# A fused LayerNorm, graph and GRU layer on one core: a planner's clock that follows tiles and loads, and a seven-product scheme in 30 batches instead of 24

## The chip, the cores and the metric

The kernel runs on 1 core of a Trainium2 chip, in one launch. The metric is device time in microseconds (us) of that core, lower is better. TensorE (PE) is the matrix engine, VectorE (DVE) and ScalarE (ACT) the elementwise engines, GpSimd (POOL) and SyncE (SP) mostly issue transfers here. "PEld" in the profile is the load of PE's stationary operand.

## What is computed

The reference, cut to what matters (32 batches of 512 rows with 256 channels, all fp32):

```python
h = maximum(layernorm(x), 0)
# inside the layer, with x standing for h:
c = relu(bn1(conv1d(xc, conv1_w)));  c = bn2(conv1d(c, conv2_w, taps=17, pad=8))
x_conv = relu(c + xc)                          # xc is x, transposed
s = x @ w_se.T + b_se                          # 3 columns
A = exp(-|s_n - s_m|^2) * adj
x_nmp = A @ relu(x @ w_msg.T + b_msg)
x_in = concat(x_conv, x_nmp)
r = sigmoid(x_in @ Wi_r + x @ Wh_r);  z = sigmoid(x_in @ Wi_z + x @ Wh_z)
n = tanh(x_in @ Wi_n + r * (x @ Wh_n))
out = x_before + (1 - z) * n + z * x
```

## The kernel before

The program is written out by Python at build time. Five generators ("streams") each yield pieces of work: `rows` (the 1x1 convolution), `begins` (LayerNorm and transposition), `graphs` (adjacency part), `conv` (the 17-tap convolution, as a fast-convolution scheme of 25 products in each of 7 groups of columns) and `gates` (the GRU). A loop at the end of the kernel function (from L1672) plays planner: it keeps a clock `now`, which is the modelled time of PE's front, and for each of ACT and DVE an `Engine` object with a modelled `free` time. A stream yields the time from which its next piece may be issued; the loop issues the piece of the stream that is furthest behind among those that are ready, adds its matmuls' modelled time to `now`, and goes on. If no stream is ready, `now` is advanced by 0.25 us, and in the early part (before the first gate batch is loaded) every fourth such empty step issues a transposition that only keeps PE busy (`keep_warm`, L147). Elementwise work with no deadline (`background`, `fill`) is issued whenever DVE's modelled backlog is under 1.5 us. All engines then run this written order[...]. The planner's times decide only the order; a wrong time shows as an engine that waits.

The clock of the version before is coarse. `Engine.issue` (L126) adds a fixed cost and a cost per element, from `max(self.free, now)`; it doesn't ask whether the inputs are there. `LAG`, 0.6 us, is added to an engine's free time wherever PE depends on it. Transfers have fixed times: a load of weights is taken to land at `now + 7.0`, of a batch's transposed rows (`load_row`) at `now + 8.0`, of a mask at no time at all.

PE's matmuls are all recorded at L137 (`matmul`), the transpositions at L142 (`turn`), the small matmuls of the adjacency kernel at L983 (`kernel_exp`), elementwise work at L128 (the `Engine` wrapper). An fp32 matmul stands as two records in the profile.

The gates of one batch are two units (`unit(o)`, o = 0, 1: halves of the output channels). A plain unit issues 18 matmuls of 512 columns: 6 each for the r, z and n gates. A "fast" unit computes the r and z products of the hidden and the convolution inputs with a seven-product scheme on halves (`term`: 7 terms of 2 matmuls of 256 columns), in place of 8 matmuls of 512, and keeps the other 10 matmuls of 512. The scheme needs sums of its data (`data_sums`, six DVE operations a batch) and of its weights (`weight_sums`, once). Within a fast unit:

- three terms fill `ps_r`'s two halves and `ps_z`'s first half; ACT copies `ps_r`'s second half to `fifth` (128x256)
- `spread(ps_r, 0)` brings `ps_z`'s first half plus `fifth` into `ps_r`'s second half
- one more term goes onto `ps_z`'s first half, and `spread(ps_z, 1)` brings that half plus `fifth` into `ps_z`'s second half
- the remaining terms and the matmuls on the graph input follow, then ACT takes tanh of `ps_r` and `ps_z`.

`spread` in the version before looks at DVE's modelled time. With `SOON = -1` it issues the sum on DVE only if DVE has been free for over 1 us. Otherwise ACT copies `ps_z`'s half, and the `fifth` is "owed": `settle_owed` adds it on DVE just before the tanh, with the tanh issued 0.2 us after that. Between the pieces stand matmuls of the unit before (`some_new`: the n gate's last four, `NEW`) and of this one (`hidden`).

Fast batches are `FIRST_FAST <= b < B - PLAIN`: with `PLAIN = 7` batches 1 to 24, so 24 of 32.

Of the kernel before, what the change touches and what calls it, by code (L numbers as in the profile page):

```python
# [13 lines left out]
P = 128  # L14
# [36 lines left out]
def kernel(  # L51
# [43 lines left out]
    const = ctx.enter_context(tc.tile_pool(name="const", bufs=1))  # L95
    front = ctx.enter_context(tc.tile_pool(name="front", bufs=2))
    cv = ctx.enter_context(tc.tile_pool(name="cv", bufs=1))
    dram = ctx.enter_context(tc.tile_pool(name="dram", bufs=1, space=bass.MemoryType.DRAM))
    acc = ctx.enter_context(tc.tile_pool(name="acc", bufs=3, space=PSUM))
    gps = ctx.enter_context(tc.tile_pool(name="gps", bufs=3, space=PSUM))  # L100
    first_ctx = ExitStack()
    cps = first_ctx.enter_context(tc.tile_pool(name="cps", bufs=2, space=PSUM))
    ctx.enter_context(tc.manual_schedule())
    late = None

    now = 5.0
    LAG = 0.6
# [6 lines left out]

    class Engine:
        def __init__(self, engine, fixed, each):
            self.engine, self.fixed, self.each, self.free = engine, fixed, each, 0.0

        def behind(self, other):
            self.free = max(self.free, other.free + 0.1)

        def __getattr__(self, name):
            def issue(*tiles, **more):
                size = max(elements(t) for t in tiles if hasattr(t, "shape"))  # L126
                self.free = max(self.free, now) + self.fixed + self.each * size
                getattr(self.engine, name)(*tiles, **more)  # L128

            return issue  # L130

    dve, act = Engine(nc.vector, 0.12, 0.00108), Engine(nc.scalar, 0.16, 0.0009)

    def matmul(ps, lhsT, rhs, **more):
        nonlocal now
        now += max(0.223, 0.005 + elements(ps) / 600.0)
        nc.tensor.matmul(ps, lhsT, rhs, **more)  # L137

    def turn(ps, a):
        nonlocal now  # L140
        now += 0.11
        nc.tensor.transpose(ps, a, ident)  # L142

    def keep_warm(n):

        for _ in range(n):
            nc.tensor.transpose(unused[:, :P], ident, ident)  # L147
# [22 lines left out]
    def store_at(t, dst, src):  # L170
        todo = [lambda: nc.gpsimd.dma_start(dst, src)]

        def run():
            if todo:
                todo.pop()()

        STORES.append(run)
        later(t, run)
# [8 lines left out]
    ARRIVES = (0.0, 7.0, 11.0, 13.0)  # L187
# [6 lines left out]
    def fetch(b, xs=None):  # L194
        XS[b] = front.tile([P, NT, D], F32, name="x_sb", bufs=2) if xs is None else xs
        step = NT // 2 if b == 0 else NT
        for c in range(0, NT, step):
            nc.sync.dma_start(
                XS[b][:, c : c + step], x[b].rearrange("(c p) d -> p c d", p=P)[:, c : c + step]
            )  # L200

    def load(b, xs=None):
# [3 lines left out]
        NORM_AT[b] = max(now + 7.0, 50.0) if b >= G else ARRIVES[b]  # L206

    def load_row(b):
        if b not in HR:
            settle_stores()  # L210
            HR[b] = front.tile([P, ND, N], F32, name="hT", bufs=2)
            nc.sync.dma_start(HR[b], HD[b])
            HR_AT[b] = now + 8.0

    def load_graph(b):
        if b < B and b not in HG and begun > b:
            settle_stores()
            HG[b] = front.tile([P, ND, N], F32, name="hTg", bufs=1)
            nc.sync.dma_start(HG[b], HD[b])

    def load_gates(b):
# [4 lines left out]
        nc.sync.dma_start(HB[b], HD[b])  # L226
        HB_AT[b] = now + 8.0

    def load_conv(b):

        if b < B and b not in XC and evacuated.get(b, 1e9) <= now:
            XC[b] = late.tile([P, ND, N], F32, name="xconv", bufs=2)
            nc.sync.dma_start(XC[b], CD[b])
            XC_AT[b] = now + 7.0
# [14 lines left out]
    def load_sums(b, d):  # L249
        if b < B and (b, d) not in XN:  # L250
            settle_stores()
            XN[b, d] = late.tile([P, N], F32, name="xnb", bufs=2)
            nc.sync.dma_start(XN[b, d], ND_[b, d])
            XN_AT[b] = now + 6.0
# [3 lines left out]
    vec = const.tile([P, _NCOL], F32)  # L258
    nc.sync.dma_start(vec, vecs)
    w1 = const.tile([P, ND, D], F32)  # L260
    nc.sync.dma_start(w1, conv1_w)

    prep_ctx = ExitStack()
    prep = prep_ctx.enter_context(tc.tile_pool(name="prep", bufs=1))
    wraw = prep.tile([P, ND, 2, 3, 3, D], F32)
    nc.gpsimd.memset(wraw[:, :, 0, 0, 0, :], 0.0)
# [3 lines left out]
    wmsg = const.tile([P, ND, D + 3], F32)  # L270
    bmsg = const.tile([P, D + 3], F32)
    ident = const.tile([P, P], F32)
    make_identity(nc, ident)
    mhalf = const.tile([P, 4], F32)
    nc.gpsimd.memset(mhalf, -0.5)

    def rsqrt(dst, var):
# [4 lines left out]
        nc.gpsimd.tensor_tensor(dst, t[:, :n], mhalf[:, :n], op=ALU.pow)  # L282
# [15 lines left out]
    h1 = const.tile([P, Q * RV], F32)  # L298
# [4 lines left out]
    def zeros(g):  # L303
        at = input_of(g)
        for b in range(B + 1):
            v = U * b - STARTS[g]
            if 0 <= v <= sizes(g)[0]:
                nc.gpsimd.memset(at[:, : Q if v == sizes(g)[0] else LEAD, :, v : v + 1], 0.0)
                if v > 0:
                    nc.gpsimd.memset(at[:, Q - 1 : Q, :, v - 1 : v], 0.0)  # L310
# [3 lines left out]
    class Graphs:  # L314


        def __init__(self):
# [6 lines left out]
            nc.gpsimd.memset(self.aug, 1.0)  # L324
            nc.gpsimd.memset(self.augr, 0.0)
            nc.gpsimd.memset(self.augl, -1.0)
# [3 lines left out]
        def ask(self, more):  # L330
# [3 lines left out]
            for k in range(self.asked, min(self.asked + more, NT * B)):  # L334
# [3 lines left out]
                if b < TURNED:  # L338
                    nc.sync.dma_start(m, adj[b, c * P : (c + 1) * P, :])
                for g in range(P // 32 if b >= TURNED else 0):  # L340
                    at = c * P + 32 * g
                    nc.sync.dma_start(
# [37 lines left out]
    def norm_some(b):  # L380

        if now < NORM_AT[b]:
# [144 lines left out]
    PLAIN = 7  # L527
# [8 lines left out]
    def weights_first():  # L536
# [10 lines left out]
        for j1 in ORDER:  # L547
# [12 lines left out]
            for j2 in ORDER:  # L560
# [7 lines left out]
                for k in range(2):  # L568
# [4 lines left out]
                    nc.scalar.dma_start(WD[len(WS)][:, k], w[k])  # L573
# [4 lines left out]
    def weights_again():  # L578


        for m in range(25, 25 * NG):
            W_BASE.append(taken)
            w = {}
            for k in (1,) if m % 25 == LONE else (2, 0, 1):
                yield
                w[k] = new_w()
                if k < 2 or m >= 50:
                    nc.sync.dma_start(w[k], WD[m % 25][:, k])
            WS.append(w)
            W_AT.append(now + 7.0)  # L590
# [10 lines left out]
    def third_weight(m):  # L601
# [5 lines left out]
        later(dve.free + 0.4, lambda: nc.gpsimd.dma_start(WD[m % 25][:, 2], w[2]))  # L607
# [103 lines left out]
    def evacuate():  # L711
# [10 lines left out]
        if g == 0 and b < 2:  # L722
# [10 lines left out]
            if o == ND - 1:  # L733
                evacuated[b] = XC_AT[b] = act.free + 0.7 + LAG
# [7 lines left out]
        act.free += 0.7  # L742
        PARTS.append(act.free + 5.0)
        n0, n1 = Q * first, min(Q * last, N)
        later(act.free + 0.4, lambda: nc.gpsimd.dma_start(CD[b][:, o, n0:n1], part[:, : n1 - n0]))
        if o == ND - 1 and last == U:
            evacuated[b] = PARTS[-1]
        return True

    AHEAD, SOON = 3, -1  # L750
# [31 lines left out]
    def prepare_some():  # L782
        nonlocal prepare_at
        if len(WS) >= 25 or len(WS) >= at_product + 3 or now < prepare_at:
# [4 lines left out]
    def convolution():  # L789
# [28 lines left out]
        for g in range(NG):  # L818
# [3 lines left out]
            if g == 1:  # L822
                first_ctx.close()
                cps = ctx.enter_context(tc.tile_pool(name="cps2", bufs=1, space=PSUM))
# [3 lines left out]
            for n in range(25):  # L828
# [6 lines left out]
                if late is None and len(WS) >= 25:  # L835
# [48 lines left out]
    def late_pools():  # L884
        nonlocal late, wih, whh, wsum, tsum
        prep_ctx.close()
        late = ctx.enter_context(tc.tile_pool(name="late", bufs=1))
        whh = late.tile([P, ND, 3 * D], F32, name="whh")
        wih = late.tile([P, 2 * ND, 3 * D], F32, name="wih")
        nc.sync.dma_start(whh, w_hh)  # L890
        nc.sync.dma_start(wih, w_ih)
# [80 lines left out]
    def kernel_exp(at):  # L972

        nonlocal now, bank_at, exp_waits
# [6 lines left out]
        for c in range(NT):  # L981
            k = slice(32 * c, 32 * c + 5)
            nc.tensor.matmul(  # L983
# [3 lines left out]
        now += 1.15  # L987
# [33 lines left out]
    def blocks(t, rows, o):  # L1021
        for g in range(P // 32):
            at = o * P + 32 * g
            nc.sync.dma_start(
# [11 lines left out]
    def begin(b):  # L1036
# [4 lines left out]
        if b >= TURNED:  # L1041
# [3 lines left out]
            nc.gpsimd.dma_start(XD_[b].rearrange("(c p) d -> p c d", p=P), xs)  # L1045
            yield now + 7.0
# [3 lines left out]
            yield now + 8.0  # L1050
# [8 lines left out]
            nc.gpsimd.dma_start(HD[b], HT[b])  # L1059
# [9 lines left out]
        for d in range(ND):  # L1069
            norm_t(b, d)  # L1070
# [6 lines left out]
    def rows(g, b):  # L1077
        nonlocal made, made_at
        for o in range(ND):
            conv1(g, b, o)  # L1080
# [5 lines left out]
    def graph(b):  # L1086
# [3 lines left out]
        if b == 0:  # L1090
            HG[0] = HT[0]
            yield act.free + LAG
        elif b not in HG:
            load_graph(b)
            yield now + 9.0
        msg = front.tile([P, NT, D], F32, name="msg", bufs=1)
        for c in range(NT):
            messages(b, msg, c)
            yield now
        told = b + 1  # L1100
        factors()
        yield dve.free + LAG
# [11 lines left out]
        for n in range(NT):  # L1114
            masked(b, at, n)
# [4 lines left out]
        for d in range(ND):  # L1120
            gather(b, msg, at, d)
# [4 lines left out]
    def gates(b):  # L1126
# [4 lines left out]
        if b < B - 1:  # L1131
            nc.sync.dma_start(out[b], x[b])
        else:
            nc.sync.dma_start(out[b][:, :P], x[b][:, :P])
# [3 lines left out]
        if b == 0:  # L1138
            yield now + 8.0
# [70 lines left out]
        def store(y, o, s):  # L1210
            for g in range(P // 32):
# [3 lines left out]
                if is_last(o):  # L1215
                    (nc.scalar if g % 2 else nc.sync).dma_start(dst, src)
                else:
                    nc.gpsimd.dma_start(dst, src, accum_op=ALU.add)  # L1218

        fast = FIRST_FAST <= b < B - PLAIN  # L1220
        if b == B - PLAIN:
            for w, at in ((whh, w_hh), (wih, w_ih)):
                nc.sync.dma_start(w[:, 0, D : 2 * D], at[:, 0, D : 2 * D])
# [484 lines left out]
```

## Time and profile before

| | |
|---|---|
| median of 3 runs (lowest to highest) | 2067.28 us (2066.85 to 2071.51) |
| profiled execution's own time, its span | 2067.35 us, 2065.6 us |
| PE, DVE, ACT, POOL busy | 2012.4, 1416.3, 888.4, 451.1 us |
| mean granted TensorE clock | 0.989 |
| DVE `ps_acc<-ps_acc,fifth`, 128x256, x96 | 41.1 us, 428 ns each |
| ACT `ps_acc<-ps_acc`, 128x256, x122 | 45.9 us, 376 ns each |
| ACT `fifth<-ps_acc`, 128x256, x48 | 18.4 us, 384 ns each |
| start of the last convolution product, of the last adjacency product (`ps_g<-at,msg`) | 1844.2, 1852.5 us of the span |

"Span" runs from the first to the last instruction on the core. A group of the page has its line, engine, operation, the tile written and those read, the shape and the count, then busy time and mean duration. The list of PE's waits names what PE waited for: the time in total, how often, and the longest single one.

### The profile page before, as it was taken

Reading aid. Unit: us, or ns where it says so; the run is one execution under the profiler, and the core shown is the slowest. Engines: PE = TensorE matmul, PEld = TensorE weight load, DVE = VectorE, ACT = ScalarE, POOL = GpSimd, SP = SyncE. Lnnn points to the kernel's source line nnn. Section 1 sums busy time; section 2 is a strip of 40 time slices with the busy share of each in tenths; the row PEclk is TensorE's granted clock in tenths of the full one; section 3 lists DMA queues with packets and bytes.
Section 4 is the critical chain, followed back from the end, with each engine's and each line's share of the span. In section 5 each row is a group of like instructions: output and inputs, shape, how many; then the busy total and the mean of one; then the engine's idle time right before and its main releaser. Section 6 shows DMA issues by size and latency. Waiting matters only on the chain. (4 is left out here: it accounts for less than half of the span.)

```text
span 2065.6 us, 27386 instructions
## 1 busy us (share of the span) xinstructions
PE 2012.4 (97%) x9199; PEld 1360.9 (66%) x9199; DVE 1416.3 (69%) x2626; ACT 888.4 (43%) x1805; POOL 451.1 (22%) x578
## 2 busy tenths in 40 slices
PE   8999889999999999999999999999999999999998
PEld 4878556676676766677577676667775677664444
DVE  6789378885878848687587775677875777752223
ACT  6554454335543445433454334554334633334221
POOL 2101022321212213122141221231221311114222
PEclk9999999999999999999999999999999999999999
DMA  7455668898979869778789788797886776756554
GB/s 286 150 174 184 225 209 196 192 226 226 223 197 203 190 192 205 201 182 212 183 193 223 172 204 206 164 197 204 207 204 175 189 158 159 173 118 143 63 92 36
DMA packets 581227, 378.70 MB, mean 183 GB/s; under 512 B 457648, under 2 KB 475344, under 8 KB 579952
## 3 DMA queue, kind: packets, MB, share of 16 engines
q1 hardware_dynamic: 419616, 279.02, 49.1%
q0 software_dynamic: 153184, 84.70, 23.9%
q10 hardware_dynamic: 8288, 13.24, 1.7%
q8 instruction: 73, 1.20, 0.2%
q14 instruction: 66, 0.54, 0.1%
HBM read 278.81 MB, written 114.56 MB: 190 GB/s over the span
## 5 line engine op out<-in xcount | busy, mean ns | idle before, releaser
L1218 POOL DMA_DIRECT2D out_dram<-o_sb x252 | 275.9, 1718 | 659.1 <-DVE o_sb L128 628.9
L137 PE MATMUL ps_acc<-xnb,wih 128*128 128x512 f32 (+1 forms) x772 | 364.4, 593 | 0.7 <-DVE ps_acc L128 0.7
L137 PEld LDWEIGHTS ps_c<-xd,w 128*128 128x128 f32 x2304 | 288.6, 191 | 55.0 <-issue 38.9
L137 PEld LDWEIGHTS ps_c<-x,w 128*128 128x128 f32 x2032 | 258.4, 193 | 72.3 <-issue 49.2
L137 PE MATMUL ps_c<-xd,w 128*128 128x135 f32 (+1 forms) x2304 | 291.8, 280 | 7.0 <-ACT ps_c L128 7.0
L137 PE MATMUL ps_c<-x,w 128*128 128x135 f32 (+2 forms) x2032 | 267.4, 281 | 11.4 <-ACT n L128 5.0
L137 PE MATMUL ps_acc<-hTb,whh 128*128 128x512 f32 (+2 forms) x580 | 239.5, 523 | 0.4 <-ACT r L128 0.4
L137 PE MATMUL ps_acc<-xconv,wih 128*128 128x512 f32 (+1 forms) x580 | 238.9, 519 | 0.3 <-DVE ps_acc L128 0.3
L137 PE MATMUL ps_g<-at,msg 128*128 128x512 f32 x512 | 227.1, 593 | 0.8 <-DVE at L128 0.8
L137 PEld LDWEIGHTS ps_acc<-xnb,wih 128*128 128x128 f32 x772 | 142.6, 191 | 115.6 <-issue 108.7
L137 PEld LDWEIGHTS ps_g<-at,msg 128*128 128x128 f32 x512 | 95.4, 190 | 106.4 <-issue 101.1
L137 PEld LDWEIGHTS ps_acc<-xconv,wih 128*128 128x128 f32 x580 | 107.6, 190 | 74.9 <-issue 67.5
L137 PEld LDWEIGHTS ps_acc<-hTb,whh 128*128 128x128 f32 x580 | 104.8, 191 | 78.6 <-issue 71.2
L128 DVE TENSOR_TENSOR msg<-ps_g,bmsg 128x256 f32<-128x256 f32 x128 | 53.7, 420 | 143.5 <-PE ps_g L137 143.1
L128 DVE SCALAR_TENSOR_TENSOR x<-x,x 128x544 f32<-128x544 f32 (+5 forms) x161 | 137.5, 854 | 2.9
L128 DVE TENSOR_TENSOR o_sb<-hTb,r 128x512 f32<-128x512 f32 x63 | 43.3, 687 | 124.1 <-ACT r L128 123.5
L128 ACT ACTIVATE ps_c<-ps_c 128x270 f32<-128x270 f32 (+1 forms) x144 | 56.1, 389 | 167.8 <-PE ps_c L137 167.8
L128 DVE TENSOR_TENSOR x<-x 128x272 f32<-128x272 f32 (+5 forms) x280 | 127.4, 497 | 0.2
L137 PE MATMUL ps_g<-hT,w 128*128 128x512 f32 (+8 forms) x296 | 122.1, 560 | 3.7 <-DMA hT<-hd 2.5
L137 PE MATMUL ps_g<-wmsg,hTg 128*128 128x259 f32 x496 | 123.5, 382 | 0.7 <-DVE aug L128 0.7
L128 ACT ACTIVATE h<-ps_g,bn_shift,bn_scale 128x252 f32<-128x252 f32 (+8 forms) x212 | 86.5, 485 | 73.2 <-PE ps_g L137 73.2
L128 DVE TENSOR_TENSOR xd<-x 128x544 f32<-128x544 f32 (+1 forms) x144 | 102.5, 716 | 14.0 <-PE ps_c L137 13.7
(149 smaller groups left out, 2927.5 us busy)
## 6 DMA issues: line engine op xcount, KB each, us to landing
w<-wd SPq DMA_DIRECT2D x414, 256.0 KB, 3.4
m_sb<-in_adj_dram SPq DMA_DIRECT2D x384, 64.0 KB, 3.8
hT<-hd SPq DMA_DIRECT2D x33, 512.0 KB, 4.4
hd<-hT POOLq DMA_DIRECT2D x32, 512.0 KB, 5.5
hTb<-hd SPq DMA_DIRECT2D x32, 512.0 KB, 4.6
xnb<-nd SPq DMA_DIRECT2D x64, 256.0 KB, 3.0
out_dram<-o_sb POOLq DMA_DIRECT2D x252, 64.0 KB, 4.9
hTg<-hd SPq DMA_DIRECT2D x31, 512.0 KB, 4.3
```

The source lines that it names most:

```text
L128: getattr(self.engine, name)(*tiles, **more)
L137: nc.tensor.matmul(ps, lhsT, rhs, **more)
L1218: nc.gpsimd.dma_start(dst, src, accum_op=ALU.add)
```

## The change

It does four things.

1. The clock. Every tile pool is wrapped in a `Pool`, every engine, POOL and SP included, in an `Engine`; each instruction and transfer records which part of which tile it wrote or read, and when that ends in the model (`note`). An instruction's modelled start is then the latest of its engine's free time and its tiles' times (`after`), PE's included (`on_pe`: `now` moves forward to the time at which operands are there). Durations have new constants. A transfer's modelled landing comes from an issue time, a latency and a shared rate (`Engine.dma_start`), and the loads' fixed 6, 7 and 8 us give way to `done(tile)`. `LAG` goes from 0.6 to 0.17.
2. The streams wait for more: for a free PSUM bank of the ring (`gps.free("ps_g")`) ahead of each use of one, for masks to have landed, for a free `hT` buffer ahead of a row load; LayerNorm pieces and weight preparation are held back while ACT's modelled backlog is over 0.5 us (`BUSY`); the late pools open when the preparation's tiles are modelled to be done within 1 us.
3. `spread` always issues the sum on DVE, at once behind the term in the program; the copy on ACT and `settle_owed` are gone.
4. `PLAIN` goes from 7 to 1: batches 1 to 30 are fast.

The diff, cut to its core:

```diff
-    now = 5.0
-    LAG = 0.6
+    now = 0.0
+    LAG = 0.17
+    BUSY = 0.5
+    HAND = 0.04
+    def after(who, outs, ins):
+        at = 0.0
+        for a in ins:
+            for k, end in met(a.tensor.name, region(a)):
+                if k[4]:
+                    at = max(at, end if k[5] == who else end + HAND)
+        for a in outs:
+            at = max(at, BORN.get(a.tensor.name, 0.0))
+            for k, end in met(a.tensor.name, region(a)):
+                if k[5] != who:
+                    at = max(at, end + HAND)
+        return at
...
     class Engine:
-        def __init__(self, engine, fixed, each):
-            self.engine, self.fixed, self.each, self.free = engine, fixed, each, 0.0
...
+        def dma_start(self, dst, src, **more):
...
+            at = max(self.free, after("DMA", [dst], [src]), lanes[0])
+            if name == "P":
+                issue = 1.1 if run < 512 else 0.78 if run == 1024 else 0.55
+            else:
+                issue = 0.53 if run < 512 else 0.43 if run == 1024 else 0.37
+            self.free = at + issue
+            rate = 150e3 if run < 512 else 330e3
+            flow = (self.free + 1.85, 4 * elements(dst) * dst.shape[0] / rate)
...
             def issue(*tiles, **more):
-                size = max(elements(t) for t in tiles if hasattr(t, "shape"))
-                self.free = max(self.free, now) + self.fixed + self.each * size
-                getattr(self.engine, name)(*tiles, **more)
+                some = [t for t in tiles if hasattr(t, "ap")]
+                given = [v for k, v in more.items() if k in ("bias", "scale") and hasattr(v, "ap")]
+                at = max(self.free, after(self.name, some[:1], some[1:] + given))
+                wide = some[0].ap[-1][0] > 8 and self.name == "ACT"
+                each = self.each * (2.2 if wide else 1.0)
+                fixed = 0.13 if op == "memset" else self.fixed
+                self.free = at + fixed + each * max(elements(t) for t in some) + 0.1 * len(given)
+                note(self.name, some[:1], some[1:] + given, self.free + self.tail)
+                getattr(self.engine, op)(*tiles, **more)
...
-    dve, act = Engine(nc.vector, 0.12, 0.00108), Engine(nc.scalar, 0.16, 0.0009)
+    dve, act = Engine("DVE", nc.vector, 0.066, 0.00106, 0.085), Engine("ACT", nc.scalar, 0.05, 0.00087, 0.12)
+    pool, sp = Engine("POOL", nc.gpsimd, 1.1, 0.0003, 0.0), Engine("SP", nc.sync, 0.0, 0.0, 0.0)
+    def on_pe(out, ins, took):
+        nonlocal now
+        now = max(now, after("PE", [out], ins)) + took
+        note("PE", [out], ins, now + 0.163)
...
-            HR_AT[b] = now + 8.0
+            HR_AT[b] = done(HR[b])
...
-        if now < NORM_AT[b]:
+        if now < NORM_AT[b] or act.free > now + BUSY:
             return False
...
-    PLAIN = 7
+    PLAIN = 1
...
-            W_AT.append(now + 7.0)
+            W_AT.append(done(*(w.values() if isinstance(w, dict) else [w])))
...
-                if late is None and len(WS) >= 25:
+                if late is None and len(WS) >= 25 and prep.over() <= now + 1.0:
                     late_pools()
...
         for c in range(NT):
+            yield gps.free("ps_g")
             messages(b, msg, c)
-            yield now
...
-                def spread(ps, k):
-                    if dve.free < now + SOON:
-                        yield max(now, fifth_at)
-                        dve.tensor_tensor(ps[:, hi], ps_z[:, lo], fifth, op=ALU.add)
-                        return dve.free + 0.3
-                    yield now
-                    act.activation(ps[:, hi], ps_z[:, lo], AF.Copy)
-                    owed.add(k)
-                    return act.free + LAG
-
-                def settle_owed(ps, k, then):
-                    if k not in owed:
-                        then()
-                        return
-                    dve.tensor_tensor(ps[:, hi], ps[:, hi], fifth, op=ALU.add)
-                    later(dve.free + 0.2, then)
+                def spread(ps):
+                    dve.tensor_tensor(ps[:, hi], ps_z[:, lo], fifth, op=ALU.add)
+                    return dve.free + LAG
...
-                r_at = yield from spread(ps_r, 0)
+                r_at = spread(ps_r)
+                yield now
...
-                z_at = yield from spread(ps_z, 1)
+                z_at = spread(ps_z)
+                yield now
...
-                yield from products(ps_z, o, 1, (2,), lambda: settle_owed(ps_z, 1, update), clear=False)
+                yield from products(ps_z, o, 1, (2,), update, clear=False)
```

## The prediction

> **What bounds the kernel now.** I read the page's busy times first, then the same busy times by stretch, PE's waits, and last the timeline at the places that they point to.
>
> ```profile
> span 2065.6 us, 27386 instructions
> ...
> PE 2012.4 (97%) x9199; PEld 1360.9 (66%) x9199; DVE 1416.3 (69%) x2626; ACT 888.4 (43%) x1805; POOL 451.1 (22%) x578
> ```
>
> PE is busy for 97% of the span: 53.2 us are idle, and no other engine comes near. So the time is PE's work, plus the idle time, plus what PE does at a reduced clock. By stretch (length, then busy time of PE, PEld, DVE, ACT, POOL, then granted clock, DMA share and GB/s):
>
> ```profile
> 0.00:52.00 52.00, 45.00 (x156) 25.84 (x157) 32.07 (x92) 32.39 (x71) 11.55 (x33) 0.93 0.77 286
> 52.00:310.00 258.00, 237.31 (x1419) 181.73 (x1419) 188.49 (x393) 132.06 (x283) 30.40 (x50) 0.96 0.56 188
> 310.00:1033.00 723.00, 707.53 (x3338) 494.10 (x3337) 546.11 (x990) 316.13 (x660) 161.06 (x210) 0.99 0.84 202
> 1033.00:1860.00 827.00, 823.45 (x3815) 569.89 (x3814) 594.07 (x1072) 354.57 (x721) 185.75 (x223) 1.00 0.79 184
> 1860.00:2014.00 154.00, 154.00 (x360) 68.27 (x359) 39.60 (x55) 43.67 (x55) 49.30 (x50) 1.00 0.59 100
> 2014.00:2066.00 52.00, 45.11 (x117) 21.10 (x116) 15.92 (x27) 9.55 (x15) 13.02 (x12) 0.98 0.41 35
> ```
>
> Idle PE, length less busy: 7.0, 20.7, 15.5, 3.6, 0 and 6.9 us. The first and last rows are loading at the start and the last unit's elementwise work; I leave both alone. What a better order can win lies between 52 and 1860 us: 39.8 us. The waits of PE from 310 to 1033 us (total, times, longest) name the releasers:
>
> ```profile
> PE ps_c L983 <- ACT z L128: 6.7, 3, 4.0
> PE ps_c L137 <- ACT ps_c L128: 3.6, 3, 3.1
> PE ps_c L137 <- ACT z L128: 1.7, 1, 1.7
> PE ps_g L137 <- DMA hT<-hd: 1.2, 1, 1.2
> ```
>
> It is ACT's evacuations, held up in ACT's own list. Two rows of ACT's waits over the whole run, and the worst place, on ACT and PE:
>
> ```profile
> ACT z L128 <- DVE ps_acc L128: 38.4, 21, 3.8
> ...
> ACT r L128 <- DVE ps_acc L128: 26.9, 13, 4.9
> ```
>
> ```profile
> 837.17 4.43 ACT L128 ACTIVATE y<-z 128x1620 f32<-128x1620 f32 x3
> ...
> 841.63 0.68 ACT L128 ACTIVATE z<-ps_c 128x270 f32<-128x270 f32 x2
> ...
> 842.37 1.22 PE L983 MATMUL ps_c<-right,left 5*128 5x512 f32 x1 [4.01 <-ACT z L128]
> ```
>
> The two rows of waits are the owed sums: ACT stands before a tanh until DVE has added `fifth`, 65.3 us in 34 cases, and everything behind it on ACT stands too. The timeline shows three copies of 1.5 us ahead of the evacuation that frees PE's bank: PE waited 4.0 us there.
>
> [...] one late sum holds ACT for up to 4.9 us. [...] behind the 4.0 us wait, at 842 us, the two pairs of small matmul rows start 1.01 us apart, against 0.53 us at 785 us, and the clock column is under 1.00 in just the stretches with waits. [...] The trace has 428 for the sum from PSUM, and I use that.
>
> **The change, part by part**
>
> *Six more fast batches.* In the timeline, two 512-column matmuls (four records) start 1.72 us before what follows, so 0.86 us each; one of 256 columns (two records) 0.43 us:
>
> ```profile
> 1103.10 0.59 PE L137 MATMUL ps_acc<-hTb,whh 128*128 128x256 f32 x2
> 1103.53 0.59 PE L137 MATMUL ps_acc<-xconv,wih 128*128 128x256 f32 x2
> ```
>
> ```profile
> 2033.13 1.88 PE L137 MATMUL ps_acc<-xnb,wih 128*128 128x512 f32 x4
> 2034.85 1.88 PE L137 MATMUL ps_acc<-hTb,whh 128*128 128x512 f32 x4
> ```
>
> A plain unit is 18 x 0.86 = 15.48 us, a fast one 14 x 0.43 + 10 x 0.86 = 14.62. Twelve units change: 12 x 0.86 = 10.3 us of PE work less. The built program agrees: 96 matmuls of 512 columns fewer, 168 of 256 more. This lies on the bound entirely, if the new units don't stall. In the old program these batches run from about 1850 us on, when convolution and adjacency have ended, so nothing else can fill a gap. I looked at the new program's order there: between the term that a sum reads and the next term on the same half always stand at least two 512-column matmuls, 1.72 us. The sum needs 0.43 us, and from PE's last start to the reader some 0.2 us (at 2034.85 PE's next group starts, ACT's tanh of the finished one at 2035.05): about 0.7 us with both hand-overs. So it is covered, with 1.0 us to spare. Ahead of it, DVE's list holds at most the three 0.69 us steps of the unit before. Added beside it: six DVE operations a batch (0.68 + 0.67 + 4 x 0.41 = 3.0 us) and 24 sums of 0.43, 28.3 us in all, in a stretch where DVE is busy 26% (39.6 of 154). Hidden; without cover at most 3.0 us a batch, 18 us, more than the 10.3 saved. No transfer is added or moved to another queue.
>
> *Sums on DVE at once.* 74 of the 96 spreads of before went over ACT. The ACT copies of 256 elements fall from 122 to 60, `fifth` rises from 48 to 60: -62 x 0.376 + 12 x 0.384 = -18.7 us of ACT, which is 43% busy, so worth nothing by itself. What counts is the 65.3 us of ACT waiting for owed sums, which delay what PE reads. In their place a DVE sum now stands at the head of DVE's list until PE's term and `fifth` are done. Queued behind it: the convolution's operand sums (`x`, `xd`), which PE needs next. Price: from nothing, where DVE is behind anyway (the planner lets it run 1.5 us behind), to about 1.7 us (two terms), 120 times. I take nothing net on PE, because DVE at 72 to 76% is itself not the bound after 310 us.
>
> *The clock, and what waits for it.* The new clock knows that an ACT copy can't start before DVE's input, and that ACT's backlog at 837 us is real; it would give PE other work there. From 310 to 1860 us idle PE is 19.0 us, and the clock of 0.99 over 723 us means up to 7 us more of reduced clock; I count 5. There is other work at all times in this stretch, so I take two thirds of 24: -16 us (bounds 0 and -24). From 52 to 310 us idle PE is 20.7 us, with some 6 us of cold clock (0.04 x 258 is 10.3, part of it inside the waits). Here DVE is 73% busy preparing weights and operands, and the new program's order shows the same want of work: 45 keep-warm transpositions against 41, and in the first 50 us of PE work only 2 us of convolution against 7. I take a quarter of 27: -7 us (bounds +8, a start as poor again as its waits suggest, and -15). The streams' new waits (PSUM bank, masks, `hT`) are the planner's, not an engine's; they cost order alone, and the same two bounds hold them. Landings taken at their modelled time in place of 6 to 8 us: the page has 3.0 to 4.6 us to land, so this lets work come earlier, at the risk of PE waiting on a late one; all DMA waits of PE now are 2.5 us. Nothing net, bounds -1 and +5.
>
> *Thinner margins.* `LAG` 0.6 to 0.17. The new program's PE list has 604 waits on ACT and 422 on DVE. Most pieces come ready well before their turn; I take +4 us (0 to 15).
>
> Sum: -10.3 - 16 - 7 + 4 = -29.3 from the profiled execution's own 2067.35 (span 2065.6 and 1.8 outside it), so 2038. The median is 2067.28, no different.
>
> **The rivals**
>
> *Only the scheme pays* (2057): the waits return elsewhere, because ACT's large copies must stand somewhere and the bound early is DVE. For it: the early order is no fuller. Against: three waits make up half of the middle's idle, and the clock now sees them. 2067.3 - 10.3 = 2057.
>
> *Everything goes* (2020): all 24 us in the middle and half of the 27 early: 2067.3 - 10.3 - 24 - 13 = 2020. Against: PE has no spare work early.
>
> *Slower* (2080): margins. PE's list holds 1026 waits on ACT and DVE; without a margin each error of the model is PE time, at that wait's place. At 0.045 us lost for each, 46 us against a gain of 33: 2080. It decides from 33.3 / 1026 = 0.032 us a wait. For it: from 1033 us on the old padding leaves hardly a wait. Against: several streams are usually ready, so a piece rarely follows its input at the earliest moment.
>
> *It does not do what it says*: the new clock errs as much as the old, and the twelve units stall as much as they save: 2067.
>
> **How the numbers follow.** Forecast (2028 to 2050) 0.52; everything goes 0.13; only the scheme 0.22; slower 0.10; nothing 0.03. 0.3%, about what a measurement of this kernel can tell from no change, is 6.2 us: faster is under 2061. Of the scheme-only case 0.19 lie there: 0.52 + 0.13 + 0.19 = 0.84 faster, 0.06 the same, 0.10 slower. The range 2018 to 2062 leaves out the slower cases and the edge of the others.
>
> **What would show it.** Right: PE busy near 2000 us; PE idle from 310 to 1860 us of some 7 us in place of 19; no `ACT z <- DVE ps_acc` row over some 10 us; no idle PE from 1860 us to the last unit. Wrong: the early stretch longer than before; hundreds of PE waits of 0.1 us on ACT and DVE; gaps before `ps_acc<-t,whh` in the last batches.

## The result and the profile after

The changed kernel takes 2048.44 us (median of 4 runs, 2045.52 to 2053.53) against 2068.56 us for the kernel before beside it: a ratio of 0.9908, 95% interval 0.9885 to 0.9930 (the two medians by themselves give 0.9903). The profiled execution took 2048.43 us, its span is 2046.7 us. 2038 was predicted, within 2018 to 2062.

The page's busy times, and the same six stretches as before (length, then busy time of PE, PEld, DVE, ACT, POOL, then the granted clock, DMA share and GB/s; the end lies 19 us earlier):

```profile
span 2046.7 us, 27748 instructions
...
PE 2002.3 (98%) x9347; PEld 1382.9 (68%) x9347; DVE 1440.9 (70%) x2686; ACT 878.0 (43%) x1755; POOL 448.2 (22%) x578
```

```profile
0.00:52.00 52.00, 44.13 (x157) 25.91 (x158) 28.21 (x90) 29.35 (x60) 12.10 (x33) 0.93 0.70 256
52.00:310.00 258.00, 248.91 (x1474) 191.96 (x1473) 206.53 (x415) 140.29 (x298) 33.10 (x54) 0.96 0.61 201
310.00:1033.00 723.00, 708.24 (x3364) 492.52 (x3363) 547.04 (x996) 313.72 (x642) 163.94 (x217) 1.00 0.84 204
1033.00:1860.00 827.00, 821.78 (x3793) 566.91 (x3792) 590.25 (x1068) 345.52 (x679) 184.65 (x222) 1.00 0.78 182
1860.00:1995.00 135.00, 134.06 (x439) 82.69 (x438) 52.64 (x92) 39.51 (x63) 41.41 (x41) 1.00 0.60 104
1995.00:2047.00 52.00, 45.19 (x127) 22.86 (x125) 16.28 (x28) 9.65 (x16) 13.02 (x12) 0.96 0.43 41
```

The span fell by 18.9 us: PE's busy time by 10.1 (2012.4 to 2002.3) and its idle time by 8.8. By stretch, idle PE went from 7.0 to 7.9 us at the start, from 20.7 to 9.1 us between 52 and 310 us, from 15.5 to 14.8 in the middle, from 3.5 to 5.2 up to 1860 us, and from 6.5 to 7.5 behind that. So almost all of the gain in idle time was made early, where a quarter of what was there had been expected, and almost none in the middle, where two thirds had been. What PE waited for from 52 to 310 us (total, times, longest), the first rows of the kernel before and then of the changed one:

```profile
PE ps_c L137 <- ACT n L128: 3.8, 3, 2.0
PE ps_c L137 <- ACT ps_c L128: 2.9, 1, 2.9
PE ps_c L137 <- ACT z L128: 2.7, 2, 1.4
PE ps_acc L983 <- ACT right L128: 2.5, 1, 2.5
```

```profile
PE ps_g L265 <- DVE augr L241: 2.1, 2, 1.7
PE ps_g L265 <- ACT at L241: 2.1, 3, 0.8
PE ps_acc L259 <- ACT right L241: 1.8, 3, 0.6
```

Over all rows of that stretch the waits on ACT fell from 16.6 to 5.9 us. PE's waits from 310 to 1033 us show new names in the place of the old ones (total, times, longest):

```profile
PE ps_c L259 <- ACT z L241: 5.1, 2, 4.3
PE ps_acc L259 <- ACT r L241: 4.3, 5, 1.6
PE ps_g L259 <- DMA hT<-hd: 1.9, 3, 1.0
PE ps_c L259 <- DVE w L241: 1.4, 1, 1.4
```

The longest, in the timeline of all engines:

```profile
348.20 0.69 DVE L241 TENSOR_TENSOR w<-w 128x512 f32<-128x512 f32 x1 [6.07 <-DMA w<-wd]
348.81 1.93 DVE L241 TENSOR_TENSOR x<-h 128x1370 f32<-128x1370 f32 x2
...
350.65 0.42 DVE L241 TENSOR_TENSOR msg<-ps_g,bmsg 128x256 f32<-128x256 f32 x1
...
351.11 0.63 ACT L241 ACTIVATE msg<-msg 128x512 f32<-128x512 f32 x1 [9.90 <-DVE msg L241]
351.64 0.66 ACT L241 ACTIVATE z<-ps_c 128x272 f32<-128x272 f32 x2
352.07 1.48 PE L259 MATMUL ps_c<-x,w 128*128 128x136 f32 x8 [4.27 <-ACT z L241]
```

DVE stood 6.1 us for weights that had not landed, at the head of its list. Behind it in that list stood the sums of `msg`, for which ACT waited 9.9 us (the next of them ran at 350.65 us, though the last record of the products that they read starts at 345.71); behind that on ACT stood the evacuation of `ps_c`, and behind that PE. That this chain, and not something beside it, holds PE can be seen in four other runs of the next section whose order is the same up to here:

| | DVE's wait for `w` | PE's wait for `z` |
|---|---|---|
| the changed kernel | 6.07 us | 4.27 us |
| clock and sums without the six batches | 5.57 | 3.77 |
| a bank asked for | 4.64 | 2.85 |
| no bank waits for the adjacency | 4.55 | 2.75 |
| the old spread under the new clock | 4.17 | 2.37 |

PE's wait is DVE's less 1.8 us in each. The wait at 837 us, which the prediction had shown, is gone, and this one has come: the clock knows of tiles now, and also relies on its model of transfers.

### The profile page after: what moved, and what is told of

Same layout as the page of the kernel before. It is cut to its first block, busy times and chain, and to the rows that moved or that the text cites. A ratio compares the mean times of both kernels' runs of the same rounds, so it can differ in the third digit from the quotient of the medians.

```text
span 2046.7 us, 27748 instructions
## 1 busy us (share of the span) xinstructions
PE 2002.3 (98%) x9347; PEld 1382.9 (68%) x9347; DVE 1440.9 (70%) x2686; ACT 878.0 (43%) x1755; POOL 448.2 (22%) x578
## 5 line engine op out<-in xcount | busy, mean ns | idle before, releaser
L259 PE MATMUL ps_acc<-hTb,whh 128*128 128x512 f32 (+2 forms) x532 | 213.1, 497 | 5.6 <-ACT r L241 5.6
L259 PE MATMUL ps_acc<-xconv,wih 128*128 128x512 f32 (+2 forms) x532 | 209.1, 495 | 1.8 <-DVE ps_acc L241 1.0
L241 DVE TENSOR_TENSOR ps_acc<-ps_acc,fifth 128x256 f32<-128x256 f32 x120 | 51.2, 427 | 204.6 <-PE ps_acc L259 188.1
L259 PEld LDWEIGHTS ps_acc<-hTb,whh 128*128 128x128 f32 x532 | 94.9, 190 | 68.6 <-issue 51.6
L259 PEld LDWEIGHTS ps_acc<-xconv,wih 128*128 128x128 f32 x532 | 98.0, 190 | 50.0 <-issue 38.8
L259 PE MATMUL ps_acc<-t,wsum 128*128 128x256 f32 x480 | 123.5, 379 | 0.8 <-DVE wsum L241 0.8
L259 PEld LDWEIGHTS ps_acc<-t,wsum 128*128 128x128 f32 x480 | 90.0, 190 | 31.3 <-issue 18.7
```

What stands on the lines that cost most here:

```text
L241: getattr(self.engine, op)(*tiles, **more)
```

## The experiments

All times are medians of runs beside the kernel before on the same chip; ratios are to that kernel, with 95% intervals. The experiments were timed in three groups, beside which the kernel before came to 2068.7, 2069.2 and 2067.5 us. The changed kernel itself was timed apart from them, with four runs between 2045.5 and 2053.5 us, so a difference from it of 2 or 3 us says little. (The planner's loop stands at L1632 of the kernel before.)

The profiles show where a written order parts from that of its parent: the first place at which DVE's or ACT's list has another operation or tile. With only `PLAIN` changed that is at about 1800 us; with another spread at about 360 us; in the runs "a bank asked for", "no bank waits" and "transfers later" at 495, 455 and 268 us; with another margin or without `BUSY` within the first 20 us. Up to that place two profiles are two executions of one order, and they show how far idle time varies by itself. From 52 to 310 us it is 20.3 to 20.7 us for the order before (four executions) and 8.4 to 9.7 us for the new one (five), so the early gain is clear. From 310 to 1033 us it varies more: 15.5 and 16.7 us for the order before, 14.8 and 19.7 for the new one. A difference of some 5 us in that stretch shows nothing.

**The scheme alone.** The kernel before, with 30 fast batches:

```diff
-    PLAIN = 7
+    PLAIN = 1
```

> The kernel before with PLAIN 7 to 1 and nothing else: six more fast batches under the old clock and the old way of bringing in the sums. Theory (the scheme is worth its PE work, whatever the clock): about 10 us less than before, so 2058. Rival (the last twelve units stall without other work to fill them, so the new sums are needed to make the scheme pay): 2063 or more, with idle PE from 1860 us on.

Measured: 2068.31 us, 0.9995 (0.9986 to 1.0003). No gain at all: the rival held. The busy time and idle time from 1860 to 2040 us, first of this run, then of the changed kernel:

```profile
1860.00:2040.00 180.00, 174.46 (x543) 101.43 (x542) 67.21 (x117) 58.44 (x93) 56.73 (x56) 1.00 0.59 93
```

```profile
1860.00:2040.00 180.00, 179.06 (x564) 105.55 (x562) 66.47 (x115) 48.79 (x78) 54.43 (x53) 1.00 0.56 88
```

5.5 us idle against 0.9. In this stretch nothing but the gates is left to issue. PE's busy time is 2005.7 us, 3.4 above that of the changed kernel, with the same matmuls apart from four transpositions that keep PE busy. The clock differs a little (0.989 against 0.991), and short waits can hide in busy time too: four records of 512 columns are shown as 1.88 us long where the next group starts 1.72 us after their start (1963.97 and 1965.69 us in this run), so by these two figures a wait of up to 0.16 us behind them would leave no gap. What ACT waits for in this run, then what PE waits for from 1860 us on:

```profile
ACT z L128 <- DVE ps_acc L128: 65.0, 33, 3.8
ACT r L128 <- DVE ps_acc L128: 29.3, 13, 4.9
```

```profile
PE ps_acc L137 <- DVE ps_acc L128: 4.2, 11, 1.2
```

46 tanh stand behind an owed sum (34 before), but that is not what holds PE. In the changed kernel PE has no wait on DVE's `ps_acc` from 1860 us on; here it has eleven. One of them, with what stands ahead of it on DVE:

```profile
1961.07 0.43 DVE L128 TENSOR_TENSOR ps_acc<-ps_acc,fifth 128x256 f32<-128x256 f32 x1 [2.67 <-PE ps_acc L137]
1961.41 0.69 DVE L128 SCALAR_TENSOR_TENSOR ps_acc<-r,ps_acc 128x512 f32<-128x512 f32 x1
...
1962.15 1.98 PE L137 MATMUL ps_acc<-xnb,wih 128*128 128x512 f32 x4 [0.26 <-DVE ps_acc L128]
```

The second line is the n gate's product with r. Its tanh had ended at 1957.46, but it stands in DVE's list behind the owed sum of `ps_z`, which waits for PE's last term; PE's next matmuls then wait for the product. All eleven are of this kind, with the tanh of r done 2.3 to 4.1 us before the product starts. While convolution is beside the gates, PE has other work in that time; in the last twelve units it has none.

**Clock and sums without the six batches.** The changed kernel with 24 fast batches:

```diff
-    PLAIN = 1
+    PLAIN = 7
```

> The changed kernel with PLAIN back at 7: the new clock and the sums on DVE, 24 fast batches. Theory: it is slower than the changed kernel by the 10 us of PE work, so some 2058 to 2059, and some 9 us faster than before, all of that from the stretch 52 to 310 us. Rival (the two parts help each other): about 2066, no different from before.

Measured: 2056.36 us, 0.9942 (0.9929 to 0.9954). 12.3 us faster than before, 8 slower than the changed kernel. Idle PE from 52 to 310 us is 9.7 us (20.7 before), from 310 to 1033 us 19.7 (15.5 before; 14.8 in the changed kernel, with the same order). The theory's place was right; the gain is larger than its 9 us, and the distance to the changed kernel smaller than its 10.

**The sums alone.** The kernel before, 24 fast batches, old clock, new spread:

```diff
-                r_at = yield from spread(ps_r, 0)
+                r_at = spread(ps_r)
+                yield now
...
-                def spread(ps, k):
-                    if dve.free < now + SOON:
...
+                def spread(ps):
+                    dve.tensor_tensor(ps[:, hi], ps_z[:, lo], fifth, op=ALU.add)
+                    return dve.free + LAG
```

> The kernel before with the sums always on DVE and issued at once, under the old clock and with 24 fast batches. Theory: ACT's waits for owed sums go (65 us), but PE gains little, since ACT is not what it waits for most: 2064 to 2069. Rival (those waits held up PE's evacuations in the middle): the idle PE from 310 to 1033 us falls from 15.5 to under 9 us, and the time to 2061 or less.

Measured: 2074.66 us, 1.0036 (1.0022 to 1.0049). Slower, outside both expectations. ACT's waits for owed sums are gone, as meant; from 310 to 1033 us idle PE is 22.8 us, and half of it has one cause:

```profile
PE ps_g L137 <- DMA hT<-hd: 11.4, 2, 6.0
PE ps_c L983 <- ACT z L128: 5.1, 2, 4.0
```

Two loads of rows came late. The old clock takes them to land at `now + 8.0`, wherever SP stands in its list. Nothing of the edit touches them; a changed order does, so how much of the 6 us is the spread's own is not shown. It is a warning for every single run here.

**Both gate parts under the old clock.** The run before this one, with `PLAIN = 1`:

```diff
-    PLAIN = 7
+    PLAIN = 1
```

> The kernel before with the new spread and PLAIN at 1: the two gate parts of the change under the old clock. Theory: against the run with the new spread alone (1.0036 of before) it gains the scheme's 8 us, so 2066 to 2067, with under 5 us lost on PE from 1860 us on. Rival (only the new clock makes the last units run without stalls): 2074, no gain over the spread alone.

Measured: 2070.71 us, 1.0009 (0.9998 to 1.0019), 4 us better than the sums alone by the medians (ratios 1.0036 and 1.0009), between the two expectations. Idle PE from 1860 to 2040 us is 2.1 us, against 5.5 with the old spread: under the old clock too the new sums take the stalls away. The middle is as bad as in the run before (26.2 us idle, with the same order there; the same two late rows make 13.8 us of the waits from 310 to 1860 us).

Three pairs of runs differ in the six batches alone, and their orders are the same up to about 1800 us. From the last operation that they share to the end, in us, with 24 and with 30 fast batches:

| | length | PE busy | PE idle |
|---|---|---|---|
| old clock, old spread | 250.8 to 250.5 | 244.0 to 238.4 | 6.8 to 12.1 |
| old clock, new spread | 254.5 to 248.4 | 247.9 to 239.7 | 6.6 to 8.7 |
| new clock, new spread | 253.9 to 247.4 | 247.3 to 238.9 | 6.6 to 8.5 |

So the six batches gain 6.1 to 6.5 us with the new spread under either clock, and 0.3 us with the old one.

**The old spread under the new clock.** The changed kernel with ACT copies and owed sums:

```diff
-                r_at = spread(ps_r)
-                yield now
+                fifth_at = act.free + 0.3
+                owed = set()
+                r_at = yield from spread(ps_r, 0)
```

> The changed kernel with the old spread: ACT copies with owed sums unless DVE has been free for 1 us; new clock, 30 fast batches. Theory (the last twelve units stall under the old spread and not under the new): some 8 us slower than the changed kernel, 2056, with about 10 us lost on PE from 1860 us on in place of 4. Rival (the stalls of the last units under the old clock came from the clock, which the new one mends): 2046 to 2050.

Measured: 2060.08 us, 0.9946 (0.9934 to 0.9959), so 11.6 us slower than the changed kernel (0.9908). From 1860 to 2040 us:

```profile
1860.00:2040.00 180.00, 174.07 (x535) 99.77 (x534) 63.87 (x110) 50.29 (x81) 54.41 (x52) 1.00 0.56 84
```

5.9 us idle. In these four runs with 30 fast batches the old spread leaves 5.5 to 5.9 us idle here under either clock, and the new one 0.9 to 2.1 (2.8 and 3.8 with the other margins below). The profiled execution, at 2053.45 us, was the fastest of six. From the place where the orders part, at 363 us, it takes 10.9 us more than the changed kernel: 5.0 us of idle time lie in this last stretch and 5.8 between 1033 and 1860 us (11.0 against 5.2), while the middle has 4.3 less (10.4 against 14.8), within what one order shows.

**The margin, old clock.** The kernel before:

```diff
-    LAG = 0.6
+    LAG = 0.17
```

> The kernel before with its margin LAG at 0.17 in place of 0.6, the coarse clock and all else as before. Theory (the margin pays only with a clock that follows the tiles; without it, PE is led into more waits): 2066 or more. Rival (the cut margin itself is what the change gains in the early stretch, and the tracking of tiles is not needed): the idle PE from 52 to 310 us falls from 20 to under 13 us and the time to 2060 or less.

Measured: 2075.93 us, 1.0023 (1.0014 to 1.0033). Slower, as the theory had it: a cut margin without a better clock leads PE into waits (idle 10.1 us from 1033 to 1860 us, against 3.5 before). Idle PE from 52 to 310 us fell to 16.5 us only, so the margin by itself is not the early gain.

**The margin, new clock.** The changed kernel with 0.6, and one list index bounded:

```diff
-    LAG = 0.17
+    LAG = 0.6
...
-                if 25 <= m + 1 < 50 and W_AT[m + 1] <= now:
+                if 25 <= m + 1 < min(50, len(WS)) and W_AT[m + 1] <= now:
```

> The changed kernel with the planner's margin LAG at its old 0.6 us in place of 0.17 (a bound on one list index is added, which changes nothing in the order at 0.17). Theory (thin margins cost at most some 4 us): 2044 to 2050. Rival (they cost as much as the middle's missing gain): 2040 or less, with the idle PE from 310 to 1860 us falling from 20 to under 10 us. A third way: waiting longer on paper delays the streams and it is slower than 2052.

Measured: 2069.53 us, 1.0002 (0.9994 to 1.0010): 21 us slower than the changed kernel, the whole gain: of the three ways expected, the third. And with less than 0.17:

```diff
-    LAG = 0.17
+    LAG = 0.05
```

> The changed kernel with LAG at 0.05 in place of 0.17. Theory (under this clock the margin is not a safety but a delay, 0.43 us more of it cost 21 us, so less costs less): 2040 to 2047. Rival (0.17 is near what a hand-over takes, below it PE is led into waits, as the old clock was by a cut margin): 2049 to 2060, with more and shorter waits of PE.

Measured: 2070.07 us, 1.0009 (0.9999 to 1.0018): 22 us slower. So the theory that the margin is a mere delay falls. The rival had the direction, but neither its number (2049 to 2060) nor its mechanism held: it expected more and shorter waits. The lists of PE's waits have 58 in 37.1 us for the changed kernel, 59 in 55.2 us at 0.05 and 60 in 48.5 us at 0.6. No more of them, but longer: at 0.05 from 310 to 1033 us these lead,

```profile
PE ps_g L259 <- DMA hT<-hd: 6.6, 4, 2.0
PE ps_acc L259 <- DVE wsum L241: 3.9, 2, 3.1
PE ps_acc L259 <- ACT r L241: 2.2, 2, 2.0
```

and the stretches show the loss early and from 1033 us on (idle 14.9, 19.0 and 10.5 us in the three long ones, against 9.1, 14.8 and 5.2; the middle one is within what one order shows by itself). Both profiled executions, 2075.9 us at 0.05 and 2072.1 at 0.6, are somewhat slower than their medians.

**A bank asked for.** The changed kernel; PE's waits on ACT's `r` looked like an accumulator bank that isn't free:

```diff
                 if o == 0 and MIXED[0] == MIXED[1]:
+                    yield acc.free("ps_acc")
                     ps_h = acc.tile([P, N], F32, name="ps_acc")
```

(and the same ahead of the other place that takes `ps_h`).

> The changed kernel in which the gates stream also waits for a free bank of the accumulator ring ahead of its n-gate matmuls, as the adjacency streams do for theirs. Theory (PE's 5.6 us of waits on ACT's tanh of r are a bank that the planner does not ask for): those waits fall under 2 us, and the time by 2 to 5 us, to 2044 to 2046. Rival (the planner has nothing better to issue there, or puts the wait elsewhere): 2047 to 2050.

Measured: 2052.69 us, 0.9924 (0.9910 to 0.9938). No gain; the waits on `r` are 4.7 us in six cases between 310 and 1860 us (4.7 in seven in the changed kernel), so the edit did not reach them. A likely reason, not tried: the tanh that frees the bank is often not written yet when the planner asks, so the ring's record doesn't know of it.

**No bank waits for the adjacency.** Six places, four of them as here and two inside a `max`:

```diff
-            yield gps.free("ps_g")
+            yield now
```

> The changed kernel with the six waits for a free bank of the adjacency ring taken out of the planner (the streams go on at once); the order is all that differs. Theory (the clock that follows the tiles makes the early gain, and these waits are a small part of it): idle PE from 52 to 310 us 8 to 13 us, time 2046 to 2053. Rival (asking for the bank is the early gain): idle PE there back to 16 us or more, 2056 or more.

Measured: 2043.41 us, 0.9885 (0.9866 to 0.9905). Idle PE from 52 to 310 us is 9.7 us, and the order is unchanged up to 455 us: there these waits change nothing, so they are not the early gain. The time is a little below the expected range, but its runs (2040.5 to 2051.6) overlap those of the changed kernel, so that the waits cost anything is not shown.

**ACT's backlog ignored:**

```diff
-    BUSY = 0.5
+    BUSY = 1e9
```

> The changed kernel with BUSY at 1e9, so that LayerNorm and weight preparation are issued whatever ACT's modelled backlog. Theory (ACT's list was clogged early: PE's early waits before were on ACT's evacuations behind other ACT work): idle PE from 52 to 310 us rises from 9.1 to 13 us or more, time 2052 or more. Rival (the rest of the clock does it): 8 to 11 us there and 2046 to 2051.

Measured: 2055.62 us, 0.9943 (0.9923 to 0.9962). The start and the early stretch:

```profile
0.00:52.00 52.00, 39.65 (x147) 24.12 (x147) 28.42 (x88) 34.02 (x75) 11.84 (x32) 0.87 0.75 275
52.00:310.00 258.00, 241.84 (x1437) 183.53 (x1436) 198.46 (x389) 130.88 (x277) 28.75 (x50) 0.97 0.57 187
```

16.2 us idle from 52 to 310 us against 9.1, and 12.4 against 7.9 ahead of that; the later stretches hardly differ (13.5 us in the middle). The profiled execution, 2051.0 us, is the fastest of six. Here an edit moved just the stretches that it was aimed at, and far beyond the 8.4 to 9.7 us that one order shows there. Without the holding back of LayerNorm and weight preparation, some 7 of the 11.6 us gained from 52 to 310 us are gone. By what path is less clear: from 52 to 310 us PE's listed waits on ACT rise only from 5.9 to 8.7 us, those on DVE from 3.0 to 3.6, and one wait of 3.6 us has no cause in the profile. The other margins, which also change the order from the start, cost 4 to 6 us there too.

**Transfers 1 us later on paper.** The changed kernel:

```diff
-            flow = (self.free + 1.85, 4 * elements(dst) * dst.shape[0] / rate)
+            flow = (self.free + 2.85, 4 * elements(dst) * dst.shape[0] / rate)
```

> The changed kernel with every modelled transfer landing 1 us later (latency 2.85 for 1.85 us in the planner's model). Theory (the largest wait that is left in the middle, 4.3 us at 352 us, stands behind DVE, which waited 6.1 us for weights that the model had landing earlier, so the model of transfers is what holds up the middle): idle PE from 310 to 1033 us falls from 14.8 to under 10 us, time 2041 to 2046. Rival (the middle's waits wander from order to order and none is owed to one term of the model): idle PE there stays at 11 to 20 us, 2046 or more.

Measured: 2040.03 us, 0.9863 (0.9848 to 0.9879): faster than both kernels, by 8 us than the changed one. Its middle and the stretch behind that:

```profile
310.00:1033.00 723.00, 712.68 (x3358) 496.85 (x3357) 540.70 (x998) 315.05 (x641) 165.43 (x218) 0.99 0.83 204
1033.00:1860.00 827.00, 819.47 (x3809) 567.90 (x3808) 597.31 (x1073) 341.76 (x681) 184.65 (x221) 1.00 0.79 182
```

Idle PE in the middle is 10.3 us (14.8), just over the expected 10, and 7.5 from there on (5.2). DVE's waits for weights in the middle are 4.4 us in place of 8.5, those for `xconv` 7.3 in place of 13.1. The gain in time is clear: the slowest of its four runs (2040.8 us) is below the fastest of the changed kernel's (2045.5). That it comes from the middle is not shown. The run with the old spread, whose model of transfers is untouched, has 10.4 us idle there; and the chain of 352 us comes back at another place, with DVE waiting 3.67 us for weights at 391 us and PE 3.49 us at 396. Of the 7.7 us between the two profiled spans, 4.3 had arisen before the orders part at all. By kind, 3.0 of them are idle time and 4.7 busy PE with the same matmuls, at a mean clock of 0.993 in place of 0.991.

## Why the prediction was right, point by point

The number came within its range partly by luck: the largest term, the middle, gave nothing, and errors of the other sign made up for half of that. Of its signs of being right, two came (PE busy 2002.3 us; no row `ACT z <- DVE ps_acc`), and a third nearly (0.9 us idle from 1860 to 2040 us); the one that stood for the middle, 7 us idle from 310 to 1860 us, did not: it was 20.0. Of its signs of being wrong, neither a longer early stretch nor hundreds of short waits came.

**Six more fast batches, -10.3.** PE's busy time fell by 10.1 us, but that agreement is chance: with 24 batches the new clock and spread have 5.6 us less of it already (2006.8 us). The six batches by themselves are worth 6.5 us in the profiles (8.4 us less busy, 1.9 more idle) and 8 us by the medians (2056.36 to 2048.44). So "lies on the bound entirely" was too much by 2 to 4 us, and the condition "if the new units don't stall" holds for the new sums alone: beside the old ones the item is worth nothing (0.9995).

**Sums at once, "nothing net on PE".** Here the prediction failed in its reasoning. It priced the copies and the waits of ACT one by one and found them off the path, which is true where there is other work. It did not ask what becomes of them in the last 180 us, where the six new batches land and no other work is left. There the owed sum is on the path, through DVE's list. The new spread is the condition for the scheme's gain: without it the changed kernel takes 11.6 us more. The order that it gave by itself, under the old clock, even cost 6.0 us (1.0036), with two late rows in it. The total did not suffer from this, because the batches had been counted with the new sums.

**The clock, middle: -16.** Measured on idle PE from 310 to 1860 us: 19.0 to 20.0, no gain, and the two other executions of these orders, 20.2 and 22.6 us, say the same. What did come is some of the reduced clock: from 310 to 1033 us it went from 0.99 to 1.00, by estimate a few microseconds of the 5 counted (0.01 of 723 us is 7), with the idle time hardly changed (15.5 and 14.8 us). The failed step is "it would give PE other work there". The named waits went, and others took their place at the same total: from 310 to 1033 us 5.1 us on ACT's `z`, of which 4.3 behind DVE's wait for a transfer, 1.9 us on rows not landed, and 4.3 us on ACT's `r`, whose cause was not found. That is the rival "only the scheme pays", true of this stretch alone.

**The clock, early: -7.** Measured: 20.7 to 9.1, -11.6. The want of work early, read from 45 keep-warm transpositions against 41 and from less early convolution, was the wrong sign to read: the waits were on ACT, 16.6 us of them, and 5.9 are left. Without the holding back (`BUSY`) 7 us of idle time return, of which the list puts 2.8 down to ACT. The 6 us counted there for the reduced clock were an estimate that took it to go with the waits. In this stretch that was not shown: from 52 to 310 us the granted clock is 0.96 with 20.7 us idle and 0.96 with 9.1.

**Landings, "nothing net, bounds -1 and +5".** PE's direct waits for transfers rose from 2.5 to 3.4 us. The item that mattered was not among those priced: a transfer that DVE waits for holds PE too, 4.3 us in the one case above.

**Thinner margins, +4 (0 to 15).** Not visible as predicted: PE has 58 listed waits in place of 46, in 37.1 us in place of 46.2, no swarm of short ones. At 0.6 us the changed kernel loses all its gain. So no cost of thin margins is shown at 0.17, and the slower rival's mechanism, so much a hand-over, was not seen even at 0.05 us. From 1033 us on, idle PE rose by 1.7 us to 1860 us and by 1.0 behind that; this is all that could be put down to it.

If the whole fall of busy PE is set against the scheme, the sum reads so: the middle 17 us too much, the early stretch 4.6 too little, the margins' 4 us not seen, and 1.9 us more idle at the start and the end that nobody had priced. That is the 10.4 us between 29.3 and the 18.9 measured on the span.

**What stays open.** The order is written greedily, and each constant changes all of it. Six edits of the changed kernel's planner gave 2040.0, 2043.4, 2052.7, 2055.6, 2069.5 and 2070.1 us. How much of the changed kernel's 20 us belongs to the clock's being right, and how much to the order that 0.17 happens to give, these runs don't tell. Nor do they tell where the 8 us of the later transfers are gained. Whether the two faster edits add up was not tried, nor was the new clock with 24 batches and the old spread.

## What to carry to other kernels

A stall that other work hides is priced at nothing only as long as that work lasts: ask of each new piece when it runs, and what is left to issue then. Where a planner writes the order, a better model moves the waits rather than removing them, and the next one may stand where the model is still optimistic: the longest here, 4.27 us, stood behind a transfer that the model had landing earlier. And two profiles of one order tell how far a stretch varies by itself; look at that before a few microseconds in it are given a cause. And before a gain is put down to a constant of a planner, try its neighbours: two of them took the whole gain away.

## What was not expected of the hardware

PE's busy time differs for the same matmuls (apart from 41, 45 and 46 keep-warm transpositions): 2005.7 us in the run of the scheme alone, 2002.3 in the changed kernel and 1997.6 in the fastest, at a granted clock of 0.989, 0.991 and 0.993. The clock alone does not explain that: the old spread under the new clock has 0.994 and 2001.5. Short waits that the records cover (1.88 us shown, 1.72 to the next start) may be the rest; how it divides is open. DVE, standing first in line for a transfer, held PE through its own list and ACT's, and what it waited beyond 1.8 us PE waited too (6.07 and 4.27 us to 4.17 and 2.37); a busy share of 70% tells nothing of that. The same transfer in the same order made DVE wait 4.17 us in one execution and 6.07 in another.
